# GRU, ternary layer and mixture of experts on one core: first weights in quarters, the first gate's seven products in another order, and matmuls of a constant ahead of them

## The chip, the cores and the metric

The kernel runs on one core of a Trainium2 chip. The metric is device time in microseconds (us) of one execution; three executions of the kernel before gave 2669.57, 2669.85 and 2670.73 us.

## The reference

Two blocks, all in f32. The first runs a GRU over 64 steps of a batch of 128, feeds its states through a layer with ternary weights and adds the input; the second runs a causal convolution whose taps are the conditioning rows, and a mixture of 64 experts with a shared expert. Only the GRU's input product matters here:

```
def cell(h, x):                       # x: 128 x 512, one step
    gi = x @ W_ih + b_ih              # 512 -> 1536: gates r, z, n
    gh = h @ W_hh + b_hh
    r = sigmoid(i_r + h_r); z = sigmoid(i_z + h_z)
    n = tanh(i_n + r * h_n)
    return (1 - z) * n + z * h
x = x + ffn(scan(cell, cond, x))      # ffn: ternary 512 x 512 weight
x = x + moe(conv(x, taps = cond))
```

## The kernel before

**The input product.** `x @ W_ih` is not multiplied out as it stands. Two steps t and t+1 are taken together, and their two 512-wide rows against the 512 columns of one gate are a 2 by 2 block product, done with seven block products (Winograd's form of Strassen) instead of eight. The blocks of x are `x11, x12` (step t, first and second half of the features) and `x21, x22` (step t+1). The blocks of a gate's weights are `w11, w12, w21, w22` (half of the features by half of the columns). One block product, `Chunk.product(n)` at L323, is two f32 matmuls of 128 by 128 by 256, and the profile records each as two, so it is "x4" in the trace, all on L338. Product 1 multiplies x11 and w11. Product 5 multiplies `s1 = x21 + x22` by `t1 = w12 - w11`, product 6 multiplies `s2 = s1 - x11` by `t2 = w22 - t1`, product 7 multiplies `x11 - x21` by `w22 - w12`, product 4 multiplies x22 by `t4 = w21 - t2`, product 3 multiplies `s4 = x12 - s2` by w22, and product 2 multiplies x12 and w21.

**Who makes the sums.** `pair_operands(t)` (L300) makes the four sums of x, on VectorE for the first pair and on GpSimd for all others. `prepare(c)` (L281) makes the four sums of gate c's weights and adds the two biases of the gate together (L294), on VectorE.

**Where the results go.** There are four PSUM tiles, `psx, psy, psw, psz`, one buffer each. Product 1 begins psx and product 2 adds to it; 7 begins psw and 4 adds to it; 5 begins psz and 3 adds to it; 6 has psy. VectorE reads each after its product: `p1` = product 1 plus the bias (L353), `u2` = product 6 plus p1 (L356), `u3` = product 7 plus half of u2 (L359), then the four quarters `gi` of the result (L361, 363, 365, 367). So product 2 can only start when p1 has been read out of psx, product 4 only when u3 has been read out of psw, and p1 needs the bias.

**The order of the work.** `input_gates()` (L369) yields one product at a time, gate by gate in the order 0, 2, 1 and within a gate in the order 1, 6, 7, 3 of the gate before, 2, 4, 5. The first 24 are taken before the recurrence begins (L448); then each step of the recurrence takes 10 or 11. On TensorE the products of the first pair are held in exactly this order (`issue_after`); all other order on each engine is laid down at build time by a planner with costs of its own, which may move an instruction ahead of others that stand before it in the text.

**The loads.** All early loads go out on SyncE's queue, in the order of the text: x of the first pair (L223, 512 KB), the weights of gate 0 in two halves of the features (L254, 512 KB each), the two biases of gate 0 repeated to 128 rows (L259, L262, 256 KB each), the weights and biases of gates 2 and 1 (1 MB a gate), the first state `h`, x of the second pair, then `whh` (1 MB a gate) and the rest. Each issue takes SyncE about half a microsecond, and each of them waits until the load eight places before it has landed: such a wait shows in the trace on SyncE's queue.

After the 24 products the recurrence runs: per step twelve f32 matmuls of the state with `whh` (L502), the gates on VectorE and ScalarE, the ternary layer of the step before (L417), and products of the pairs ahead in between. Once, ahead of the first of these layers, VectorE turns the ternary weights into signs (L457 to L471), for which `wf` must have landed.

Of the kernel before, what the change touches and what calls it, by code (L numbers as in the profile page):

```python
# [8 lines left out]
F32 = mybir.dt.float32  # L9
# [5 lines left out]
ALU = mybir.AluOpType  # L15
# [4 lines left out]
P = 128  # L20
B = 128
T = 64
D = 512
# [19 lines left out]
def adaln_ffn_kernel(  # L43
# [156 lines left out]
    with (  # L200
# [21 lines left out]

        load_pair(0, nc.sync)  # L223
        h = el0.tile([P, D], F32, name="h")
# [16 lines left out]
        bi = wi.tile([P, 3 * D], F32, name="bi")  # L241
        wih = [wi.tile([P, KD, D], F32, name=f"wih{c}") for c in range(3)]

# [7 lines left out]

        for h_ in range(2):
            half_ = slice(h_ * HD, (h_ + 1) * HD)
            load_rows(wih[0][:, h_ * HK : (h_ + 1) * HK], w_ih[half_, cols[0]])  # L254
        bh = {}
        for c in (0, 2, 1):
            if c:
                load_rows(wih[c], w_ih[:, cols[c]])
            repeated(bi[:, cols[c]], b_ih[cols[c]])  # L259
            if c != 2:  # L260
                bh[c] = el0.tile([P, D], F32, name="r")
                repeated(bh[c], b_hh[cols[c]])  # L262
        nc.sync.dma_start(out=h, in_=cond)
        load_pair(2, nc.sync)
# [10 lines left out]
        nc.vector.memset(ones, 1.0)  # L275

        wsum = {}

        def prepare(c):  # L281

            w = wih[c]
            w11, w12 = w[:, :HK, :HD], w[:, :HK, HD:]
            w21, w22 = w[:, HK:, :HD], w[:, HK:, HD:]
            t1 = wi.tile([P, HK, HD], F32, name=f"t1{c}")
            nc.vector.tensor_sub(t1, w12, w11)
            t2 = wi.tile([P, HK, HD], F32, name=f"t2{c}")
            nc.vector.tensor_sub(t2, w22, t1)  # L289
            nc.vector.tensor_sub(w12, w22, w12)  # L290
            t4 = wi.tile([P, HK, HD], F32, name=f"t4{c}")
            nc.vector.tensor_sub(t4, w21, t2)
            if c in bh:
                nc.vector.tensor_add(bi[:, cols[c]], bi[:, cols[c]], bh[c])  # L294
            wsum[c] = {1: w11, 2: w21, 3: w22, 4: t4, 5: t1, 6: t2, 7: w12}

        gis, last = {}, []
        made = []

        def pair_operands(t):  # L300

            xp = xps.pop(t)
            x11, x12 = xp[:, 0, :HK], xp[:, 0, HK:]
            x21, x22 = xp[:, 1, :HK], xp[:, 1, HK:]
            s = xpp.tile([P, 3, HK, B], F32, name="xs")
            s1, s2, s4 = s[:, 0], s[:, 1], s[:, 2]
            engine = nc.gpsimd if t else nc.vector
            engine.tensor_add(s1, x21, x22)
            engine.tensor_sub(s2, s1, x11)
            engine.tensor_sub(x21, x11, x21)  # L310
            engine.tensor_sub(s4, x12, s2)
            return {1: x11, 2: x12, 3: s4, 4: x22, 5: s1, 6: s2, 7: x21}

        class Chunk:


            def __init__(self, t, c, ops):
                self.c, self.ops, self.ws = c, ops, wsum[c]
                self.g = [gip.tile([P, 2, HD], F32, name="gi") for _ in range(2)]
                gis[t, c], gis[t + 1, c] = (g.rearrange("p h d -> p (h d)") for g in self.g)  # L320
                self.ps = {}

            def product(self, n):  # L323
# [33 lines left out]
                elif n == 7:  # L357
                    self.u3 = gtp.tile([P, HD], F32, name="u3")
                    add(self.u3, ps, self.u2[:, 1])  # L359
                elif n == 5:  # L360
                    add(g1[:, 1], ps, self.u3)  # L361
# [7 lines left out]
        def input_gates():  # L369
# [1111 lines left out]
```

## Time and profile before

| what | value |
|---|---|
| median of three runs (lowest, highest) | 2669.85 us (2669.57, 2670.73) |
| the profiled execution's own time | 2670.76 us |
| its span, first to last instruction | 2669.0 us |
| TensorE busy with matmuls | 2639.1 us, 99% |
| VectorE, ScalarE, GpSimd busy | 1412.3, 426.3, 458.0 us |
| first product of the input (L338) starts | 5.99 us |
| first matmul of the recurrence (L502) starts | 34.26 us |

The profile is of one execution. Its page shows the busy time of each engine, and the trace can be asked for the instructions of a stretch in order of time (the timeline), for the busy time of each engine in given stretches (the windows), and for the chain of waits that ended last. In a timeline row stand the start and the length in us, the engine, the line of the kernel, the operation, what it writes and reads, the shape, and how many instructions were merged; in brackets how long the engine stood idle before and what ended it. "PEld" is the load of the stationary operand, "SPq" is SyncE issuing a transfer. The ends of matmuls are modelled, so that rows of TensorE overlap a little.

### The profile page before, as it was taken

Reading aid. Unit: us, or ns where it says so; the run is one execution under the profiler, and the core shown is the slowest. Engines: PE = TensorE matmul, PEld = TensorE weight load, DVE = VectorE, ACT = ScalarE, POOL = GpSimd, SP = SyncE. Lnnn points to the kernel's source line nnn. Section 1 sums busy time; section 2 is a strip of 40 time slices with the busy share of each in tenths; the row PEclk is TensorE's granted clock in tenths of the full one; section 3 lists DMA queues with packets and bytes.
Section 4 is the critical chain, followed back from the end, with each engine's and each line's share of the span. In section 5 each row is a group of like instructions: output and inputs, shape, how many; then the busy total and the mean of one; then the engine's idle time right before and its main releaser. Section 6 shows DMA issues by size and latency. Waiting matters only on the chain.

```text
span 2669.0 us, 31315 instructions
## 1 busy us (share of the span) xinstructions
PE 2639.1 (99%) x11959; PEld 1818.0 (68%) x11959; DVE 1412.3 (53%) x3148; ACT 426.3 (16%) x795; POOL 458.0 (17%) x534
## 2 busy tenths in 40 slices
PE   8999999999999999999999999999999999999999
PEld 5666666666666666666658667777876666666667
DVE  6555555555555555555547655566574343434334
ACT  1111111111111111111110222222221111111111
POOL 2112121111112111211114100000001222222210
PEclk9999999999999999999999999999999999999999
DMA  5323332332322222322228811222256899998962
GB/s 193 69 56 63 57 67 57 58 61 53 60 47 51 44 52 44 75 45 58 48 67 294 324 25 26 39 61 60 61 169 174 287 305 294 288 330 262 293 182 48
DMA packets 476054, 323.35 MB, mean 121 GB/s; under 512 B 329472, under 2 KB 395648, under 8 KB 473728
## 3 DMA queue, kind: packets, MB, share of 16 engines
q1 hardware_dynamic: 447312, 248.18, 33.3%
q0 software_dynamic: 28592, 73.16, 11.3%
q8 instruction: 95, 1.56, 0.2%
q14 instruction: 55, 0.45, 0.1%
HBM read 235.01 MB, written 92.55 MB: 123 GB/s over the span
## 4 chain that ended last, share of the span: by engine, by line
PE 93%; issue 2%; DMA 2%; DVE 2%; ACT 0%; SPq 0%; POOL 0%; DVEq 0%; POOLq 0%; ACTq 0%
PE psgh L502 25%; PE psz L695 7%; PE psw L695 7%; PE psx L695 6%; PE psw L338 6%; PE psz L338 6%; PE psx L338 6%; PE psf L417 4%; PE py L1370 3%; PE y L695 3%; PE psy L338 3%; PE pg L1344 3%; PE pu L1344 3%; PE psc L182 2%; PE y L869 1%
## 5 line engine op out<-in xcount | busy, mean ns | idle before, releaser
L502 PE MATMUL psgh<-whh,hT 128*128 128x512 f32 x1536 | 676.3, 597 | 0.7 <-ACT hT L399 0.7
L502 PEld LDWEIGHTS psgh<-whh,hT 128*128 128x128 f32 x1536 | 287.5, 190 | 351.0 <-issue 336.9
L338 PE MATMUL psx<-wih,xp 128*128 128x256 f32 x768 | 198.5, 381 | 6.4 <-DMA wih<-in_w_ih_dram 6.0
L220 POOL DMA_DIRECT2D xn<-in_x_dram x61 | 33.9, 555 | 842.4 <-DVE x L428 830.8
L338 PEld LDWEIGHTS psx<-wih,xp 128*128 128x128 f32 x768 | 143.8, 191 | 25.6 <-issue 6.0
L512 DVE TENSOR_TENSOR n<-psgh,bhn 128x512 f32<-128x512 f32 x64 | 44.2, 691 | 175.2 <-PE psgh L502 175.2
L1353 DVE SCALAR_TENSOR_TENSOR a<-a,rw,pu 128x352 f32<-128x352 f32 x32 | 18.6, 580 | 215.1 <-PE pu L1344 215.1
L399 ACT COPY hT<-psf 128x512 f32<-128x512 f32 x64 | 37.5, 585 | 584.2 <-PE psf L393 584.2
L509 DVE TENSOR_TENSOR r<-psgh,gi 128x512 f32<-128x512 f32 x64 | 44.2, 691 | 142.5 <-PE psgh L502 142.5
L413 POOL TENSOR_TENSOR xn<-xn,fb 128x512 f32<-128x512 f32 x64 | 80.8, 1263 | 144.1 <-DMA xn<-in_x_dram 144.1
L338 PE MATMUL psz<-wih,xs 128*128 128x256 f32 x384 | 98.7, 380 | 1.8 <-DVE gi L361 1.8
L338 PE MATMUL psy<-t,xs 128*128 128x256 f32 x384 | 99.9, 383 | 0.4 <-DVE t L289 0.3
L338 PE MATMUL psw<-t,xp 128*128 128x256 f32 x384 | 98.8, 380 | 0.4 <-DVE u L359 0.4
L338 PE MATMUL psw<-wih,xp 128*128 128x256 f32 x384 | 98.8, 380 | 0.0
L338 PE MATMUL psz<-t,xs 128*128 128x256 f32 x384 | 98.7, 379 | 0.0
L417 PE MATMUL psf<-sgn,hhi 128*128 128x512 f32 x256 | 95.1, 493 | 0.3 <-DVE hlo L407 0.3
L1370 PE MATMUL py<-wd,aeT 128*64 128x512 f32 (+1 forms) x384 | 89.5, 601 | 0.0
L353 DVE TENSOR_TENSOR p<-psx,bi 128x512 f32<-128x512 f32 x96 | 66.4, 691 | 37.5 <-PE psx L338 37.2
L515 ACT ACTIVATE n<-n 128x512 f32<-128x512 f32 x64 | 40.3, 629 | 274.0 <-DVE n L514 274.0
L695 PE MATMUL psx<-hid,swg 128*128 128x256 f32 x320 | 83.7, 384 | 0.3 <-ACT g L735 0.3
L695 PE MATMUL psx<-xr,swg 128*128 128x256 f32 x320 | 83.6, 383 | 0.0
L356 DVE TENSOR_TENSOR u<-psy,p 128x512 f32<-128x512 f32 x96 | 66.3, 691 | 29.4 <-PE psy L338 29.1
(306 smaller groups left out, 4678.4 us busy)
## 6 DMA issues: line engine op xcount, KB each, us to landing
wg<-in_w_gate_dram SPq DMA_DIRECT2D x64, 704.0 KB, 9.6
wu<-in_w_up_dram SPq DMA_DIRECT2D x64, 704.0 KB, 11.0
wd<-in_w_down_dram SPq DMA_DIRECT2D x64, 512.0 KB, 7.0
x1c<-x SPq DMA_DIRECT2D x62, 256.0 KB, 5.2
out_dram<-x SPq DMA_DIRECT2D x62, 256.0 KB, 5.4
xn<-in_x_dram POOLq DMA_DIRECT2D x61, 256.0 KB, 4.1
xp<-in_xT_dram POOLq DMA_DIRECT2D x30, 512.0 KB, 5.2
xc<-x1c SPq DMA_DIRECT2D x28, 512.0 KB, 8.3
```

The costliest lines, as they stand in the source:

```text
L182: i = nc.tensor.matmul(ps[rows, j].rearrange("p h (u t) -> p h u t", u=2), xcs[sl % NCB][:, rows, g * 4 + j], tzs[sl % NCB][:, :, :, g * 4 ...
L338: i = nc.tensor.matmul(ps, self.ops[n][:, k, :], self.ws[n][:, k, :], start=(first and k == 0), stop=(k == HK - 1), skip_group_check=not f ...
L353: add(self.p1, both, b)
L356: add(self.u2, both, self.p1)
L413: nc.gpsimd.tensor_add(xn, xn, fb)
L417: nc.tensor.matmul(ps, piece[:, k, :], sgn[:, k, :], start=(i == 0 and k == 0), stop=(i == 1 and k == KD - 1),)
L502: nc.tensor.matmul(ps, hT[:, k, :], whh[c][:, k, :], start=(k == 0), stop=(k == KD - 1))
L509: nc.vector.tensor_add(r, ps_r, gis.pop((t, 0)))
L512: nc.vector.tensor_add(n, ps_n, bhn)
L695: i = nc.tensor.matmul(ps.rearrange("p (j b) -> p j b", b=P) if len(r.shape) == 3 else ps, lhs(k), r, start=(first and k == 0), stop=(k == ...
L1344: nc.tensor.matmul(acc[halves[j]], self.xeT[:, k, halves[j]], self.ws[j][which][:, k, :], start=(k == 0), stop=(k == KD - 1),)
L1370: nc.tensor.matmul(py[halves[j]], self.aeT[:n, c, halves[j]], self.ws[j][2][:n, c, :], start=(c == 0), stop=(c == len(ech) - 1),)
```

## The change

Four edits, all of them at the start of the kernel.

1. The loads that gate 0 needs go out in nine pieces in place of five: x11 (128 KB), w11 (256 KB), x of the second step (256 KB), w12, w22 (256 KB each), the two biases, x12 (128 KB), w21 (256 KB). The four quarters of gate 0's weights are tiles of their own, `wb`. Biases now stand ahead of x12 and w21. Everything behind keeps its order.
2. Seven 128 by 128 by 128 matmuls of `ones` with itself are put ahead of the first product. Nothing reads their result.
3. In the first gate the products run in the order 1, 5, 6, 7, 2, 4. As product 5 now comes before u3 exists, its PSUM tile is kept (`p5`), and the quarter that used to be added at product 5 is added behind u3 at product 7.
4. VectorE's sums for that gate are held in the order s1, t1, s2, t2, x11 - x21, w22 - w12, the bias, s4, t4, where the four sums of x came first before.

```diff
-        load_pair(0, nc.sync)
+        xps[0] = xpp.tile([P, 2, KD, B], F32, name="xp")
...
-        for h_ in range(2):
-            half_ = slice(h_ * HD, (h_ + 1) * HD)
-            load_rows(wih[0][:, h_ * HK : (h_ + 1) * HK], w_ih[half_, cols[0]])
+        def load_block(k, n):
+            load_rows(wb[k, n], w_ih[k * HD : (k + 1) * HD, n * HD : (n + 1) * HD])
...
+        nc.sync.dma_start(out=xps[0][:, 0, :HK], in_=xT[0, :, :HK])
+        load_block(0, 0)
+        nc.sync.dma_start(out=xps[0][:, 1], in_=xT[1])
+        load_block(0, 1)
+        load_block(1, 1)
+        load_biases(0)
+        nc.sync.dma_start(out=xps[0][:, 0, HK:], in_=xT[0, :, HK:])
+        load_block(1, 0)
+        for c in (2, 1):
+            load_rows(wih[c], w_ih[:, cols[c]])
+            load_biases(c)
...
+        ps = ps_f.tile([P, D], F32, name="psf")
+        for _ in range(7):
+            nc.tensor.matmul(ps[:, :P], ones, ones, start=True, stop=True)
...
+            todo = [
+                (t1, w12, w11, ALU.subtract),
+                (t2, w22, t1, ALU.subtract),
+                (w12, w22, w12, ALU.subtract),
+                (t4, w21, t2, ALU.subtract),
+            ]
             if c in bh:
-                nc.vector.tensor_add(bi[:, cols[c]], bi[:, cols[c]], bh[c])
+                b = bi[:, cols[c]]
+                todo.insert(3, (b, b, bh[c], ALU.add))
+            if c == 0:
+
+                x1, x2, x7, x4 = xsums
+                todo = [x1, todo[0], x2, todo[1], x7, *todo[2:4], x4, todo[4]]
+            for operands in todo:
+                with tc.issue_after(summed[-1].ins) if c == 0 and summed else nullcontext():
+                    summed.append(nc.vector.tensor_tensor(*operands))
...
                 elif n == 7:
                     self.u3 = gtp.tile([P, HD], F32, name="u3")
                     add(self.u3, ps, self.u2[:, 1])
+                    if self.p5 is not None:
+                        add(g1[:, 1], self.p5, self.u3)
+                elif n == 5 and "psw" not in self.ps:
+                    self.p5 = ps
                 elif n == 5:
                     add(g1[:, 1], ps, self.u3)
...
-                    for n in (1, 6, 7, 3, 2, 4, 5):
+                    for n in (1, 6, 7, 3, 2, 4, 5) if prev else (1, 5, 6, 7, 2, 4):
```

More of the change, by code (lines that the diff above doesn't have):

```diff
@@ L241, in adaln_ffn_kernel @@
         bi = wi.tile([P, 3 * D], F32, name="bi")
-        wih = [wi.tile([P, KD, D], F32, name=f"wih{c}") for c in range(3)]
+        wb = {
+            (k, n): wi.tile([P, HK, HD], F32, name=f"w{k}{n}") for k in range(2) for n in range(2)
+        }
+        wih = {c: wi.tile([P, KD, D], F32, name=f"wih{c}") for c in (1, 2)}
         xc0 = xcs[0].rearrange("p b e -> p (b e)")
@@ L248, in repeated, with load_biases @@
             nc.sync.dma_start(out=dst, in_=row.partition_broadcast(P))
-        for h_ in range(2):
-            half_ = slice(h_ * HD, (h_ + 1) * HD)
-            load_rows(wih[0][:, h_ * HK : (h_ + 1) * HK], w_ih[half_, cols[0]])
+        def load_block(k, n):
+            load_rows(wb[k, n], w_ih[k * HD : (k + 1) * HD, n * HD : (n + 1) * HD])
         bh = {}
-        for c in (0, 2, 1):
-            if c:
-                load_rows(wih[c], w_ih[:, cols[c]])
+        def load_biases(c):
             repeated(bi[:, cols[c]], b_ih[cols[c]])
@@ L275, in adaln_ffn_kernel @@
         nc.vector.memset(ones, 1.0)
+        ps = ps_f.tile([P, D], F32, name="psf")
+        for _ in range(7):
+            nc.tensor.matmul(ps[:, :P], ones, ones, start=True, stop=True)
         wsum = {}
         def prepare(c):
[L283 to L292, printed above, removed]
-            if c in bh:
-                nc.vector.tensor_add(bi[:, cols[c]], bi[:, cols[c]], bh[c])
+            if c == 0:
+                w11, w12, w21, w22 = (wb[k, n] for k in range(2) for n in range(2))
+            else:
+                w = wih[c]
+                w11, w12 = w[:, :HK, :HD], w[:, :HK, HD:]
+                w21, w22 = w[:, HK:, :HD], w[:, HK:, HD:]
+            t1, t2, t4 = (wi.tile([P, HK, HD], F32, name=f"t{n}{c}") for n in (1, 2, 4))
+            todo = [
[4 more added lines that the diff above has]
+            ]
+            if c in bh:
+                b = bi[:, cols[c]]
+                todo.insert(3, (b, b, bh[c], ALU.add))
+            if c == 0:
+                x1, x2, x7, x4 = xsums
[3 more added lines that the diff above has]
+                    summed.append(nc.vector.tensor_tensor(*operands))
             wsum[c] = {1: w11, 2: w21, 3: w22, 4: t4, 5: t1, 6: t2, 7: w12}
         gis, last = {}, []
-        made = []
+        made, summed, xsums = [], [], []
         def pair_operands(t):
@@ L306, in pair_operands @@
             s1, s2, s4 = s[:, 0], s[:, 1], s[:, 2]
[L307 to L311, printed above, removed]
+            todo = [
+                (s1, x21, x22, ALU.add),
+                (s2, s1, x11, ALU.subtract),
+                (x21, x11, x21, ALU.subtract),
+                (s4, x12, s2, ALU.subtract),
+            ]
+            if t == 0:
+                xsums.extend(todo)
+            else:
+                for operands in todo:
+                    nc.gpsimd.tensor_tensor(*operands)
             return {1: x11, 2: x12, 3: s4, 4: x22, 5: s1, 6: s2, 7: x21}
@@ L320, in __init__ @@
                 gis[t, c], gis[t + 1, c] = (g.rearrange("p h d -> p (h d)") for g in self.g)
-                self.ps = {}
+                self.ps, self.p5 = {}, None
             def product(self, n):
```

## The prediction

> **What bounds the kernel now.** The page comes first: its table of engines and its slices say whether a gain at the start can reach the end.
>
> ```profile
> PE 2639.1 (99%) x11959; PEld 1818.0 (68%) x11959; DVE 1412.3 (53%) x3148; ACT 426.3 (16%) x795; POOL 458.0 (17%) x534
> ...
> PE   8999999999999999999999999999999999999999
> ```
>
> TensorE is without matmuls for 2669.0 - 2639.1 = 30 us in all, and its first slice is the weakest. So the start is a fair target, and what TensorE gains there comes out at the end unless another engine takes it back. The profiled execution took 2670.76 us, 1.8 over its span and 0.9 over the median of the runs; I count in its trace and take the difference off the median.
>
> The timeline of the first 15 us comes next, to see what TensorE waits for.
>
> ```profile
> 5.94 0.68 DVE L287 TENSOR_TENSOR t<-wih 128x512 f32<-128x512 f32 x1
> ...
> 5.99 2.05 PE L338 MATMUL psx<-wih,xp 128*128 128x256 f32 x4 [5.99 <-DMA wih<-in_w_ih_dram]
> ...
> 8.33 2.07 PE L338 MATMUL psy<-t,xs 128*128 128x256 f32 x4 [0.29 <-DVE t L289]
> ...
> 10.40 0.69 DVE L294 TENSOR_TENSOR bi<-bi,r 128x512 f32<-128x512 f32 x1 [0.93 <-DMA r<-in_b_hh_dram]
> ...
> 11.94 1.13 PE L338 MATMUL psx<-wih,xp 128*128 128x256 f32 x4 [0.37 <-DVE p L353]
> ...
> 13.27 1.13 PE L338 MATMUL psw<-t,xp 128*128 128x256 f32 x4 [0.19 <-DVE u L359]
> 14.24 1.03 PE L338 MATMUL psz<-t,xs 128*128 128x256 f32 x4
> ```
>
> Two things are seen. A product takes 2.05 us at first and 1.03 later (0.86 from one to the next): TensorE starts at half its rate. And what ends the last waits is not the weights: the bias lands at 10.3, and behind it stand four steps on VectorE, one after the other (bias 10.40, p1 11.20, u2 11.99, u3 12.79), before product 4 may start at 13.27. The chain of waits says the same of the bias:
>
> ```profile
> 2.83 7.48 DMA r<-in_b_hh_dram
> ```
>
> Last the windows, for who is the bound behind that point.
>
> ```profile
> 10.00:15.00 5.00, 4.44 (x17) 3.19 (x17) 3.99 (x8) 0.00 (x0) 0.00 (x0) 1.00 1.05 399
> 15.00:20.00 5.00, 5.00 (x24) 4.10 (x23) 5.00 (x10) 0.00 (x0) 0.00 (x0) 1.00 1.05 367
> 20.00:25.00 5.00, 5.00 (x24) 4.07 (x22) 4.67 (x8) 0.00 (x0) 3.72 (x4) 1.00 1.05 391
> ```
>
> After the stretch stand TensorE, its weight loads, VectorE, ScalarE, GpSimd, the clock, the busy share of the DMA engines and GB/s. From 15 to 25 VectorE is as full as TensorE (5.00 and 4.67 of 5), and so are the DMA engines. That decides my forecast.
>
> **Part by part.** *Smaller loads.* The same 2 MB go out ahead of gate 2's weights as before. The first issue is at 0.81, the next ones half a microsecond apart, so nine issues last until 0.81 + 9 x 0.5 = 5.3; the DMA engines move 256 KB in about 0.7 us (360 to 400 GB/s), so they are not starved. Product 1 needs 384 KB instead of the 1024 KB that landed at 5.85. In the trace x's 512 KB had landed at 4.4, and w11 is issued second, at 1.31: I take 4.1 for it, between 3.5 (384/512 of the bytes behind a start at 1.8) and 5.85 (nothing gained). w12 and w22 follow at 0.7 us each, some 5.6 and 6.3. The price is the length of the runs: quarters of the weights and halves of x move in runs of 1 KB. The trace's packet records have 84 ns as the median for 2 KB and 48 for 1 KB, so 1 KB costs 6 ns more per KB on each of 16 engines: for 1280 KB that is 1280 x 6 / 16 = 0.5 us on everything behind. It lies in the slack of later loads (the wait for `wf` ends at 36.6, and VectorE stands idle there because the result is only wanted with the matmuls that end at 41.3).
>
> The page "DMA: Bandwidth & Descriptors" of the Trainium skill (section Bandwidth) speaks against small pieces: batch transfers to 1 MiB, as 1 MB reaches 341 GB/s and 64 KB only 138. By it a 256 KB piece would get some 240 GB/s (an estimate between the page's two figures), and the bias would land 2 us later, not earlier. The windows decide against it: with transfers of 256 KB to 1 MB queued behind one another the rows above have 367 to 399 GB/s.
>
> *The bias.* It now has 1152 KB ahead of it instead of 1536. At 390 GB/s that is 1.0 us earlier, less 0.3 for the runs of 1 KB: 9.65 instead of 10.31. The bounds are 8.6 and 10.8, since the trace's window rows show only 90 to 119 GB/s from 7.5 to 9.0, while the bias moves; whether this belongs to the bias or to the moment isn't shown.
>
> *Seven matmuls of ones.* `ones` is written at 0.91 and ready at 1.1. A product's 256 columns start 0.43 us apart at the slow rate, so 128 columns take 0.21: 14 records x 0.21 = 3.0 us, 1.15 to 4.15. They end about where w11 lands, so they cost nothing if it lands at 4.1, and at most 0.6 if it lands at 3.5. What they bring is product 1, 5, 6 or 7 at the full rate. But all four stand ahead of a wait for the bias, so even slow ones are done in time: 4.2 + 1.7, then 5 from 6.4 (t1), 6 and 7, 1.7 each, to 11.5. I take nothing for it, and 0.9 as the most (one product at the full rate).
>
> *The order 1, 5, 6, 7, 2, 4.* Product 5 no longer follows product 4, which takes 0.86 us of TensorE out of the stretch behind 13.27. The four products that need no bias are done by about 9.2 at the full rate (5 behind t1 at 6.3, 6 behind t2 at 7.4, 7 behind w22 - w12 at 8.3). Then TensorE waits for p1. In place of a wait for weights there is one for the bias of some 2 us, and queued behind product 2 are all the products of gate 2.
>
> *VectorE.* s4 and t4 used to be done before the bias came; now x12 and w21 land behind it, and the two sums cost 0.34 + 0.60 = 0.94 us behind it. That is the hidden price. With the bias at 9.65 the chain to u3 ends 0.66 earlier, at 12.6. The two sums go in behind it or into it, so VectorE stands where it stood before at 13.5 instead of 13.2: -0.66 + 0.94 = 0.28 later. It wins back the 0.29 that it waited for product 4 at 14.44. Sum for VectorE: 0.0. The added sum for product 5 replaces one that was there.
>
> *The sum.* TensorE is ahead by 0.86 + 0.66 = 1.5 us when gate 2 begins. If VectorE, full from 15 to 25, hands on u3 of gate 1 at 25.9 as before, nothing of it is left at the product that waits for it at 26.37. If TensorE's lead is kept, 1.5 is. The row nearest is VectorE's 5.00 of 5.00, but it also holds 1.0 us in which two of its sums took 1.12 and 1.21 instead of 0.68, beside GpSimd's, and that can move either way. I take the middle, -0.7: 2669.85 - 0.7 = 2669.1 us. About 0.2% (5.3 us) is what a measurement of this kernel can tell from no change, and this is far less.
>
> **The rivals.** *A: the wait for the bias throws the clock back.* The trace has one such place, in the windows at the end of the recurrence:
>
> ```profile
> 1390.00:1391.00 1.00, 0.00 (x0) 0.00 (x0) 1.00 (x3) 0.00 (x0) 0.00 (x0) 1.00 0.00 0
> 1391.00:1392.00 1.00, 0.45 (x4) 0.42 (x4) 0.50 (x1) 0.00 (x0) 0.00 (x0) 1.00 0.08 8
> 1392.00:1393.00 1.00, 0.32 (x3) 0.12 (x2) 0.00 (x0) 0.72 (x2) 0.00 (x0) 1.00 0.87 91
> ...
> 1394.00:1395.00 1.00, 1.00 (x2) 0.33 (x1) 0.21 (x1) 0.00 (x0) 0.00 (x0) 0.50 0.85 130
> ```
>
> Waits of 1.65 and 0.68 us close together, with TensorE busy for 0.77 of 3 us (26%), were followed by 3.4 us at half the clock, a loss of 1.7 us. The new kernel has a wait of some 2.2 us from 9.2 to 11.4. It decides if TensorE is busy for a quarter or less of the stretch the clock is judged by; with products 6 and 7 in front I count 35 to 50%. The price is 1.7 for one period: 2669.85 - 0.7 + 1.7 = 2670.9, slower than before, and 2672.6 with two.
> The page "TensorE: Matmul & The Clock Gate" of the Trainium skill (sections What you observe, HAM oscillation) says full clock comes after about 3.4 us of steady work, is judged in windows of that length that run freely, and is lost by idle gaps over 3.4 us. By it this wait would be harmless; the rows above show a loss after 1.65 and 0.68, so I keep the rival.
>
> *B: the front comes through whole.* If the biases move at the 390 GB/s of the rows around them, they land 1.0 us earlier still; then TensorE's lead is 2.5 us, and if the planner uses it to shorten the 1.8 us wait of psz for VectorE at 49.7, 4.3. That gives 2669.85 - 2.5 = 2667.3 to 2665.5. Against it stands VectorE's full row; past -5.3 it would need more of the waits behind 13.27 to go.
>
> *C: the planner lays the rest out anew.* The order on every engine comes from its costs, and the start shifts them. The price is that of the waits there are behind 14 us: 30 - 6.0 - 1.0 = some 23 us, in pieces of up to 1.8. Three such pieces more or fewer are 5.4: 2664.5 or 2675.3. Nothing in the profile tells the sign.
>
> *D: no smaller waits.* If the pieces land together, as the queue interleaves them, product 1 starts near 5.9 still, and 0.5 us of short runs remain: 2670.3.
>
> **How the numbers follow.** Forecast 0.36; A 0.14 (0.03 of it past +0.2%); B 0.20 (half of it past -0.2%); C 0.24 (0.05 faster, 0.09 slower past the bound); D 0.06. Faster by over 0.2%: 0.10 + 0.05 = 0.15. Slower: 0.03 + 0.09 = 0.12. Within: 0.73. The range leaves out some 0.09 on each side: past B's and C's lower ends by one more piece of 1.8, 2663.0, and past C's upper end by the half microsecond of short runs, 2676.0. The forecast's own range is -1.5 - 0.9 to +0.6: 2667.4 to 2670.5.
>
> **What would show it.** Right: product 1 at full rate near 4.2; products 1, 5, 6, 7 done near 9.2; a bias step on VectorE near 9.7; product 4 near 13 and gate 2's first product near 14 instead of 14.9; and then VectorE full to 26, with the first matmul of the recurrence within 1.5 us of 34.26. The forecast is wrong if L502 starts before 32.5, if a row of the first 20 us has a clock of 0.50 behind product 7, or if the traces part behind 35 us by more than they did there.

## The result, and the profile after

The changed kernel takes 2674.2 us (median of 18 runs, 2671.19 to 2677.79), the kernel before, run beside it, 2670.25 (18 runs, 2667.65 to 2673.29). The ratio is 1.0015, with a 95% interval of 1.0009 to 1.0021. It is slower, by some 4 us. That is inside the 0.2% that I set as the bound of a difference, but the interval excludes no change, and the forecast was 0.7 us faster.

The profiled execution took 2675.57 us, its span is 2673.9. Its page begins with the table of engines:

```profile
PE 2643.0 (99%) x11973; PEld 1819.2 (68%) x11973; DVE 1409.6 (53%) x3148; ACT 426.7 (16%) x795; POOL 457.5 (17%) x534
```

TensorE has 14 instructions more, the matmuls of ones. It starts 4.9 us earlier and is still without matmuls for 30.9 us (2673.9 - 2643.0), where it was for 30: the idle time has come back elsewhere. The timeline of the start shows where:

```profile
1.13 3.35 PE L294 MATMUL psf<-ones 128*128 128x128 f32 x14 [1.13 <-DVE ones L290]
...
4.28 1.75 PE L374 MATMUL psx<-w,xp 128*128 128x256 f32 x4
...
6.95 1.13 PE L374 MATMUL psz<-t,xs 128*128 128x256 f32 x4 [0.92 <-DVE t L324]
...
8.86 1.10 PE L374 MATMUL psw<-w,xp 128*128 128x256 f32 x4
...
10.67 0.69 DVE L324 TENSOR_TENSOR bi<-bi,r 128x512 f32<-128x512 f32 x1 [1.90 <-DMA r<-in_b_hh_dram]
...
11.28 0.41 DVE L324 TENSOR_TENSOR xs<-xp,xs 128x256 f32<-128x256 f32 x1
11.61 0.68 DVE L389 TENSOR_TENSOR p<-psx,bi 128x512 f32<-128x512 f32 x1
...
12.21 0.68 DVE L324 TENSOR_TENSOR t<-w,t 128x512 f32<-128x512 f32 x1
...
12.35 1.92 PE L374 MATMUL psx<-w,xp 128*128 128x256 f32 x4 [2.39 <-DVE p L389]
...
12.81 0.68 DVE L392 TENSOR_TENSOR u<-psy,p 128x512 f32<-128x512 f32 x1
13.60 0.42 DVE L395 TENSOR_TENSOR u<-psw,u 128x256 f32<-128x256 f32 x1
...
14.08 2.04 PE L374 MATMUL psw<-t,xp 128*128 128x256 f32 x4
```

Product 1 starts at 4.28, 5 at 6.95, 7 at 8.86 as meant, though product 1 doesn't have the full rate yet (1.75 us). Then TensorE stands for 2.39 us. The bias step on VectorE comes at 10.67, not at 9.65 and not even at 10.40 as before; between it and u3 now stand s4 (11.28) and t4 (12.21). And product 2 takes 1.92 us instead of 1.13: the clock has gone. The chain of waits still names the same transfer:

```profile
3.73 6.85 DMA r<-in_b_hh_dram
```

The clock is granted in stretches that begin and end on a grid of 3.41 us; the trace lists them, and where the grid lies differs from one execution to the next. The windows, asked for on this execution's grid (after the stretch: length, busy TensorE, weight loads, VectorE, ScalarE, GpSimd, clock, DMA share, GB/s):

```profile
5.72:9.13 3.41, 2.49 (x11) 1.65 (x10) 2.56 (x5) 0.00 (x0) 0.25 (x1) 1.00 0.55 208
9.13:12.55 3.42, 1.03 (x5) 0.58 (x4) 1.88 (x4) 0.00 (x0) 0.00 (x0) 1.00 1.03 388
12.55:15.96 3.41, 3.41 (x9) 2.35 (x9) 2.72 (x6) 0.00 (x0) 0.00 (x0) 0.50 1.05 388
15.96:19.37 3.41, 3.07 (x15) 2.41 (x14) 3.11 (x6) 0.00 (x0) 0.00 (x0) 1.00 0.94 297
```

In the second row TensorE is busy for 1.03 of 3.42 us, 30%; the third row then has half the clock although TensorE is full in it. Such a stretch is called a fall from here on.

A second place differs, near 49 us, inside the first step of the recurrence. It is the wait of psz for VectorE that rival B had its eye on. The timelines of TensorE there, before and then after:

```profile
42.84 0.28 PE L462 MATMUL psf<-total,ones 128*128 128x1 f32 x2
42.98 1.96 PE L502 MATMUL psgh<-whh,hT 128*128 128x512 f32 x4
...
49.72 1.10 PE L338 MATMUL psz<-wih,xs 128*128 128x256 f32 x4 [1.76 <-DVE gi L361]
```

```profile
44.58 0.28 PE L502 MATMUL psf<-total,ones 128*128 128x1 f32 x2
44.72 1.10 PE L542 MATMUL psgh<-whh,hT 128*128 128x512 f32 x2
...
51.46 1.10 PE L374 MATMUL psz<-w,xs 128*128 128x256 f32 x4 [2.62 <-DVE gi L401]
```

`psf<-total` sums the absolute ternary weights over the partitions; VectorE's signs wait for it, and VectorE's work for the products waits behind the signs. The planner has put that small matmul behind one more matmul of the recurrence: 4 records (two matmuls) stood behind it before, 2 (one) now. VectorE is that much later, and the wait grew from 1.76 to 2.62 us.

### The profile page after: what moved, and what is told of

It is laid out like the page before. It is cut to its first block, busy times and chain, and to the rows that moved or that the text cites. A ratio compares the mean times of both kernels' runs of the same rounds, so it can differ in the third digit from the quotient of the medians.

```text
span 2673.9 us, 31354 instructions
## 1 busy us (share of the span) xinstructions
PE 2643.0 (99%) x11973; PEld 1819.2 (68%) x11973; DVE 1409.6 (53%) x3148; ACT 426.7 (16%) x795; POOL 457.5 (17%) x534
## 4 chain that ended last, share of the span: by engine, by line
PE 92%; DMA 3%; DVE 2%; issue 2%; ACT 0%; SPq 0%; POOL 0%; DVEq 0%; POOLq 0%; ACTq 0%
PE psgh L542 25%; PE psz L735 7%; PE psw L735 7%; PE psx L735 6%; PE psw L374 6%; PE psz L374 6%; PE psx L374 6%; PE psf L457 4%; PE py L1410 3%; PE y L735 3%; PE psy L374 3%; PE pg L1384 3%; PE pu L1384 3%; PE y L909 1%; PE psf L433 1%
## 5 line engine op out<-in xcount | busy, mean ns | idle before, releaser
L374 PE MATMUL psx<-wih,xp 128*128 128x256 f32 x512 | 131.5, 379 | 0.0
L374 PEld LDWEIGHTS psx<-wih,xp 128*128 128x128 f32 x512 | 97.3, 190 | 13.8 <-DVE p L389 0.4
L550 ACT ACTIVATE r<-r 128x512 f32<-128x512 f32 x64 | 40.3, 630 | 260.9 <-DVE r L549 260.9
L374 PEld LDWEIGHTS psw<-t,xp 128*128 128x128 f32 x384 | 73.1, 191 | 12.2 <-DVE u L395 1.1
```

The lines of the kernel that those rows point to most:

```text
L374: i = nc.tensor.matmul(ps, self.ops[n][:, k, :], self.ws[n][:, k, :], start=(first and k == 0), stop=(k == HK - 1), skip_group_check=not f ...
L550: nc.scalar.activation(r, r, AF.Sigmoid)
```

## The experiments

All are read by the same marks in the profile: the bias step on VectorE, product 2, the first matmul of the recurrence, `psf<-total`, the first matmul of the third step, and the stretches of half clock ahead of 1390 us. Times in us; the median of the runs stands beside the ratio to the kernel before (11 runs of each kernel, 18 for the first row of after; single runs have no ratio).

| kernel | bias | product 2 | recurrence | total | third step | half clock from | median | ratio (95%) |
|---|---|---|---|---|---|---|---|---|
| before | 10.40 | 11.94 | 34.26 | 42.84 | 77.32 | none | 2670.25 | 1 |
| b_again | 10.02 | 11.56 | 33.84 | 42.43 | 76.91 | none | 2669.47 | 0.9996 (0.9987 to 1.0005) |
| b_again2 | 10.31 | 12.01 | 34.06 | 42.65 | 77.11 | none | 2668.11 (one) | |
| after | 10.67 | 12.35 | 35.14 | 44.58 | 79.06 | 12.55 | 2674.2 | 1.0015 (1.0009 to 1.0021) |
| e0_again | 10.72 | 12.41 | 34.71 | 44.15 | 79.69 | 51.41 | 2674.4 | 1.0012 (1.0003 to 1.0021) |
| a_p3 | 11.06 | 12.75 | 36.05 | 45.49 | 81.05 | 15.04, 52.59 | 2675.53 (one) | |
| a_p4 | 10.76 | 12.45 | 34.20 | 43.64 | 78.12 | none | 2673.52 (one) | |
| e1_fill | 10.32 | 12.03 | 33.77 | 43.21 | 77.71 | none | 2672.26 | 1.0008 (0.9999 to 1.0017) |
| u_warm | 10.84 | 12.52 | 34.28 | 43.72 | 78.21 | none | 2672.87 | 1.001 (1.0 to 1.0019) |
| u_loads | 10.57 | 12.86 | 35.22 | 42.95 | 77.43 | none | 2670.65 | 0.9999 (0.999 to 1.0008) |
| e3_bias | 12.24 | 15.20 | 35.74 | 42.61 | 77.59 | 7.78 (twice as long) | 2671.97 | 1.0005 (0.9996 to 1.0014) |
| e4_bias_pe | none | 11.31 | 31.41 | 40.93 | 76.06 | none | 2673.21 | 1.001 (1.0001 to 1.0019) |
| e2_two | 10.98 | 12.66 | 34.44 | 43.13 | 82.23 | 14.49, 52.03 | 2674.68 | 1.0013 (1.0004 to 1.0022) |
| e2_three | 10.97 | 12.65 | 33.64 | 43.18 | 82.34 | 12.36, 53.32 | 2676.14 | 1.0015 (1.0006 to 1.0024) |
| e6_fill_both | 11.14 | 12.83 | 34.58 | 44.03 | 78.50 | none | 2671.26 | 1.0002 (0.9993 to 1.0011) |
| b_fill2 | 10.27 | 12.11 | 33.71 | 42.29 | 76.78 | none | 2669.82 | 1.0 (0.9991 to 1.0009) |
| e5_defer | none | 13.03 | 32.74 | 43.12 | 75.43 | 8.66 | 2668.89 | 0.9995 (0.9986 to 1.0004) |
| b_defer | 10.07 | 11.62 | 33.84 | 44.14 | 74.31 | none | 2668.62 | 0.9992 (0.9983 to 1.0001) |

The kernel before, run beside them, had medians of 2670.58, 2670.63, 2670.58 and 2670.77 in the four groups of runs. The medians of equal kernels differ by 1.1 us (b_again against the kernel beside it), so what is worth less than that is read from the marks. The half clock is given as the trace lists it; where no row is shown, the windows show it in the same way as above.

The mean granted clock of every single execution is on record too, rounded to thousandths. One fall takes half of 3.41 us, 0.0006 of the span, so 0.999 stands for one or two falls and 0.998 for two or more, the one at the end of the recurrence included. In the four later groups the kernel before has 1.000 in 49 of 114 executions (median 2669.84) and 0.999 in the other 65 (2671.28). The changed kernel (after and e0_again together) never has 1.000: 0.999 in 12 executions (2673.06), 0.998 in 17 of 29 (2674.76).

### The changed kernel again: e0_again, a_p3, a_p4

No edit.

> The changed kernel once more, for what scatters from one execution to the next. Its profile had the clock at half from 12.55 to 15.96 us, the first matmul of the recurrence (psgh) at 35.14 against 34.26 before, the third step's at 79.06 against 77.32, and another 2.7 us between 1441 and 1530. Theory: the first 1.7 us (to the third step) belong to the change and come again within 0.3, except that the half clock may fall elsewhere, since the stretch that it is judged by need not begin at the same place; the 2.7 us are scatter and need not come again. Rival: the 2.7 us belong to the change and come again within 0.3. Time against the kernel before: +2 to +5 us either way.

> The changed kernel, a third profile. Theory: a half clock behind the wait for the bias or behind the one near 49 us; third step at 78.7 to 80.0; from the first psc to the first pst of the 21st group 132.3 to 136.1 (kernel before: 132.3 to 133.4 in three profiles), so overlapping. Rival: 134.4 or more in every profile.

> The changed kernel, a fourth profile, with the same expectations.

The clock was thrown back at the first wait in one execution (after), at the wait near 49 in one (e0_again), at both in one (a_p3) and at neither in one (a_p4). The windows on the grids of e0_again and of a_p4:

```profile
48.00:51.41 3.41, 0.79 (x4) 0.39 (x4) 3.41 (x8) 1.23 (x2) 0.00 (x0) 1.00 0.15 36
51.41:54.82 3.41, 3.41 (x10) 2.66 (x9) 3.41 (x8) 0.63 (x1) 0.00 (x0) 0.50 0.06 14
```

```profile
8.73:12.14 3.41, 1.54 (x7) 0.87 (x5) 1.73 (x4) 0.00 (x0) 0.00 (x0) 1.00 1.04 375
12.14:15.55 3.41, 2.51 (x10) 1.92 (x11) 3.27 (x8) 0.00 (x0) 0.00 (x0) 1.00 1.04 385
46.27:49.69 3.42, 1.64 (x8) 1.11 (x6) 3.42 (x7) 0.20 (x1) 0.00 (x0) 1.00 0.16 38
49.69:53.10 3.41, 2.49 (x9) 1.62 (x10) 3.41 (x8) 1.66 (x3) 0.00 (x0) 1.00 0.09 20
```

a_p4 has the same waits, 2.17 and 2.62 us. But its grid cuts both in two, and no window falls under 1.54 of 3.41 (45%). The third step was expected at 78.7 to 80.0 and came at 81.05 and 78.12: two falls and none. In e0_again the first wait is another: the full clock came only at 10.45, in spite of the matmuls of ones, so products 5 and 6 took 2.08 and 1.78 us and the wait for the bias was 0.84. The stretch behind the recurrence was expected to overlap with the kernel before, or else to be 134.4 or more in every profile; with 134.2 and 134.9 neither came out whole (below).

e0_again shows one more thing: no fall at the front, but its recurrence starts 0.51 later than a_p4's, with the bias step at the same time. VectorE's timelines, of e0_again and then of a_p4, say where:

```profile
22.48 1.23 DVE L324 TENSOR_TENSOR bi<-bi,r 128x512 f32<-128x512 f32 x1
23.64 1.21 DVE L324 TENSOR_TENSOR t<-wih,t 128x512 f32<-128x512 f32 x1
```

```profile
22.52 0.69 DVE L324 TENSOR_TENSOR bi<-bi,r 128x512 f32<-128x512 f32 x1
23.12 1.22 DVE L324 TENSOR_TENSOR t<-wih,t 128x512 f32<-128x512 f32 x1
```

Beside GpSimd's sums, two of VectorE's are stretched in e0_again and one in a_p4, and the 0.54 us pass through to the recurrence. All three profiles of before have two (the first by 0.44, 0.42 and 0.34), and so has a_p3 (by 0.31).

With that taken out, the way from the bias step to the first matmul of the recurrence is 23.40 to 23.42 us in the three profiles of before and 23.44 in the two of after without a fall at the front (e0_again, a_p4), as it is, to 0.01, in e1_fill, u_warm and e6_fill_both further down. Against 23.44 a fall at the front costs 1.03 (after: 35.14 - 10.67 - 23.44) and 1.24 (a_p3). From there to the third step it is 43.92 where no fall lies near 49, and 44.98 and 45.00 where one does: 1.06 and 1.08. From the recurrence's start to `total` it is 9.44 in all four, and 8.58 or 8.59 before: 0.86 by the planner.

### Keeping TensorE busy in the wait: e1_fill

```diff
+                            if t == 0 and c == 0 and n == 2:
+                                for _ in range(10):
+                                    with tc.issue_after(made[-1].ins):
+                                        made.append(
+                                            nc.tensor.matmul(ps[:, :P], ones, ones, start=True, stop=True)
+                                        )
```

> Ten more matmuls of ones between product 7 and product 2 of the first gate, so that TensorE isn't idle while it waits for the bias. Theory (wait and clock): no half clock behind 10 us; products 2 and 4 at 0.9 to 1.1 us instead of 1.9 and 2.0; the first psgh 0.8 to 1.7 us earlier than in the changed kernel, so 33.4 to 34.3; the time 1 to 2 us below the changed kernel's. Rival (VectorE is the bound from 15 to 25 us, as I forecast): the clock holds, but the first psgh stays at 35.1 within 0.2 and the time does not move.

```profile
9.80 2.39 PE L426 MATMUL psf<-ones 128*128 128x128 f32 x20
12.03 1.11 PE L374 MATMUL psx<-w,xp 128*128 128x256 f32 x4
13.74 1.13 PE L374 MATMUL psw<-t,xp 128*128 128x256 f32 x4 [0.60 <-DVE u L395]
```

Products 2 and 4 run at 1.11 and 1.13 instead of 1.92 and 2.04, there is no fall, and the median is 2.1 us under e0_again in the same group of runs. The matmuls add work and take time away, so what they repair is the clock; the record of the single executions says the same, with 0.998 in 2 of 11. Against the kernel before, run beside it, 1.7 us are left.

### Which edit makes the wait: u_warm, u_loads

u_warm has no matmuls of ones at the start (`range(0)` for `range(7)`); everything else is the changed kernel. u_loads has the loads of the kernel before (x in one load, gate 0's weights in two halves of the features) with the other three edits.

> The changed kernel without its seven matmuls of ones; the planner leaves the order of everything else as it was. Theory (the warming makes the wait that loses the clock): products 1, 5, 6, 7 run at half rate, 1.7 us each, and end near 11.5 instead of 9.7; the wait for p1 shrinks to 1 us, no half clock comes behind full clock before 20 us, products 2 and 4 run at the full rate or nearly, first psgh at 33.7 to 34.7 instead of 35.14 and 34.71, the time 0 to 1.5 us below the changed kernel's. Rival (warming is what holds the front up): slow products delay u2 and u3, first psgh at 35.5 or later, the time 1 us above.

> The changed kernel with the loads of the kernel before (x whole, gate 0's weights in two halves of the features, then the biases); warming, product order and VectorE's order stay, the transposes of the first state are held behind the 24 products. Theory: product 1 at 5.9, product 5 near 6.8, the bias at 10.3 as before, so the wait between product 7 and product 2 is there too (products 1, 5, 6, 7 done by 9.7, product 2 at 12.3) and the first psgh comes at 34 to 35: the loads are not what costs. Rival (the loads cost: runs of 1 KB, the bias 0.3 us later): first psgh at 33.5 or earlier and the time at or under the kernel before.

u_warm:

```profile
8.81 1.91 PE L374 MATMUL psy<-t,xs 128*128 128x256 f32 x4
10.52 1.69 PE L374 MATMUL psw<-w,xp 128*128 128x256 f32 x4
12.52 1.13 PE L374 MATMUL psx<-w,xp 128*128 128x256 f32 x4 [0.32 <-DVE p L389]
```

Left at half rate, products 5, 6 and 7 last until the bias is there: the wait is 0.32 instead of 2.39, product 2 starts within 0.2 us of the same time, and the clock holds from 11.85 on. The median is 1.3 under the changed kernel, little more than the 1.1 between equal kernels, but the clock is 0.999 in all 11 executions, where the changed kernel had 0.998 in 17 of 29. So the matmuls of ones bring nothing, as predicted, and in many executions they cost: they let the products end early, and the wait that this makes is what throws the clock back. The wait near 49 (2.6 us) is still there, and a fall at it was not met in this profile.

u_loads has a wait of 2.20 us too, for the same bias, so the small loads alone don't make it. There VectorE makes s4 and t4 both ahead of p1, which puts product 2 2.29 us behind the bias step instead of 1.68. Its product 1 is 1.7 us later than in after, and its recurrence starts at 35.22, but the planner put `psf<-total` 7.73 us behind that instead of 9.44, and the third step is at 77.43. It equals the kernel before, and this says more of that one placement than of the loads. No run has the old order of products or of VectorE's sums with the new loads, so edits 3 and 4 weren't taken apart.

### The bias: e3_bias, e4_bias_pe

In e3_bias the two bias loads go out right behind w11. In e4_bias_pe they are two rows of 2 KB, and one matmul of ones over these 2 rows both adds them and spreads them over 128 rows. Both hold the transposes of h behind the products, an order that the planner may change without that.

```diff
         load_block(0, 0)
+        brow = w0.tile([2, D], F32, name="brow")
+        nc.sync.dma_start(out=brow[0:1], in_=b_ih[cols[0]].unsqueeze(0))
+        nc.sync.dma_start(out=brow[1:2], in_=b_hh[cols[0]].unsqueeze(0))
...
-        load_biases(0)
...
+                                    made.append(
+                                        nc.tensor.matmul(psb, ones[0:2], brow, start=True, stop=True)
+                                    )
+                                    nc.scalar.copy(bi[:, cols[0]], psb)
```

> The changed kernel with the biases of gate 0 loaded right behind w11 instead of behind w22, and the transposes of the first state held behind the 24 products (where they stand in the changed kernel). Theory (the wait for the bias is what breaks the front): the bias step on VectorE at 7 to 8.5 us instead of 10.7, product 2 started by x12 and w21 at 10.5 to 11, no wait of TensorE over 1.7 us behind product 5, no half clock behind 10 us; first psgh 0.7 to 1.7 us earlier than the changed kernel's 35.14, so 33.4 to 34.4. Rival: the bias loads move at some 100 GB/s wherever they stand, so x of the second step, w12 and w22 land 2 us later each, products 5, 6 and 7 with them, and the first psgh stays at 35.1 within 0.3.

> The changed kernel with gate 0's two biases not repeated to 128 rows by the load: two rows of 2 KB are loaded, and one matmul of ones over those two rows puts their sum in PSUM behind product 1, from where ScalarE copies it. VectorE's bias sum for that gate goes, 512 KB of loads go. Theory: x12 and w21 land near 9, products 1, 5, 6, 7, 2, 4 follow each other with no wait over 1 us behind product 5; gate 2's first product starts between 11.5 and 13.5 instead of 15.9; first psgh at 32 to 33.5; time 1.5 to 3 us below the changed kernel's. Rival (VectorE is full from there on): gate 2's first product comes early but the first psgh not before 34.3.

Why is the bias later though 384 KB fewer stand ahead of it? Where the biases move, the DMA engines carry little more than 100 GB/s. Before that is at 7 to 9 us (211 and 102 GB/s), in the changed kernel at 7 to 9 too, and in e3_bias it moves with them to 4 to 6 (windows of after, then of e3_bias):

```profile
7.00:8.00 1.00, 1.00 (x5) 0.74 (x6) 1.00 (x3) 0.00 (x0) 0.00 (x0) 1.00 0.25 100
8.00:9.00 1.00, 1.00 (x6) 0.74 (x6) 0.77 (x2) 0.00 (x0) 0.00 (x0) 1.00 0.56 205
```

```profile
4.00:5.00 1.00, 1.00 (x6) 0.91 (x5) 0.00 (x0) 0.00 (x0) 1.00 (x2) 1.00 0.58 100
5.00:6.00 1.00, 0.41 (x2) 0.01 (x1) 0.00 (x0) 0.00 (x0) 0.96 (x1) 1.00 0.99 100
```

In e4_bias_pe, where gate 0 has no repeated load, no microsecond from 2 to 9 is under 219 GB/s:

```profile
6.00:7.00 1.00, 1.00 (x3) 0.50 (x2) 0.61 (x2) 0.00 (x0) 0.00 (x0) 1.00 1.10 313
7.00:8.00 1.00, 1.00 (x5) 0.53 (x4) 1.00 (x3) 0.47 (x1) 0.00 (x0) 1.00 0.88 240
8.00:9.00 1.00, 1.00 (x6) 0.86 (x5) 1.00 (x3) 0.11 (x1) 0.00 (x0) 1.00 0.89 332
```

So most of the slowness belongs to these loads and not to the moment, which the prediction had left open. Not all of it: in halves of a microsecond e4_bias_pe has 141 and 135 GB/s from 3.5 to 4.5 us, and e5_defer, with the same loads, 115 and 82. Why the biases take longer than before isn't told by this alone; the landings further down say a little more.

In e3_bias all that stands behind the biases comes late (VectorE's first sum at 8.92, product 5 at 10.50), which is worse at the front: the recurrence starts at 35.74, later than the theory and the rival had it. Only the early placement of `psf<-total` (6.87 us behind the first matmul of the recurrence) brings the third step back to 77.59, and the median, 2671.97, with it.

e4_bias_pe has the front that the change was supposed to bring: product 2 at 11.31 behind a wait of 1.01, gate 2's first product at 13.96, no fall, and the third step 1.05 us ahead of the mean of before. The recurrence's start at 31.41 flatters it, as 1.5 products (1.3 us) had been put behind it. The runs didn't follow: 2673.21, in two groups, 2670.75 to 2672.33 and 2673.21 to 2675.22. The expected time was missed. Part of the loss is the clock, which is 0.999 in the quicker executions but for one and 0.998 or 0.997 in six others. The front isn't the same in each execution either: e5_defer, which has it too, shows product 2 at 13.03 and a fall at 8.66. The rest is open; in the profile, of one of the quicker executions, the stretch behind the recurrence is the longer one again.

### The place of `psf<-total`: e2_two, e2_three

In both, `psf<-total` is held by hand behind two or three of the third gate's four matmuls, and the products of the first step behind all four. This takes three products out of the stretch ahead of the recurrence, so that its start can't be compared with the other rows.

> The changed kernel with the one matmul that adds up the ternary weights' size (psf<-total) held behind two psgh matmuls of the third gate, where it stood before the change; the products of the stream that the planner puts beside it are held behind all psgh of the first step. To be read against e2_three. Theory: that matmul starts 0.8 to 0.9 us earlier than in e2_three, the signs on VectorE too, TensorE's wait for gi behind it is shorter by as much (1.8 against 2.6), and so is everything from the second step on: 0.85 us less time. Rival: VectorE's chain of signs isn't what TensorE waits for, and the two differ by less than 0.3 us at the third step.

> The same with that matmul held behind three psgh matmuls of the third gate, where the planner put it in the changed kernel. Theory: 0.85 us more than e2_two at the third step and in the time. Rival: within 0.3 of e2_two.

From the first matmul of the recurrence to `total` it is 8.69 against 9.54, and to the second step 27.36 against 28.29: one matmul later costs 0.93 us there, as expected. The third step shows none of it (82.23 against 82.34), since the fronts happened to differ by 0.8 the other way. Both have two falls, and their third step is 1.2 us later than a_p3's, which has two as well; what holding the products adds to this can't be told apart. TensorE's longest wait there is 2.7 us in the one and 3.5 in the other. The pair supports the price only with the front taken off.

### The wait near 49: e6_fill_both, b_fill2

e6_fill_both is e1_fill with 8 more matmuls of ones ahead of product 3 of the second pair's gate 2, where the wait near 49 stands. b_fill2 is the kernel before with 6 at its own wait there.

> e1_fill (ten matmuls of ones in the wait for the bias) with eight more in the wait of 2.6 us for gi near 49 us. Theory (the half clock that follows a wait is what most of the loss is, and which wait it follows differs from one execution to the next): no half clock before 1390 us in the profile; first psgh at 33.8, third step's at 77.7 within 0.3, as in e1_fill's profile; the time 0.3 to 1.5 us under e1_fill's and within 1 us of the kernel before. Rival (the rest of the loss lies behind the recurrence): the time stays at e1_fill's +1.7 within 0.5.

> The kernel before with six matmuls of ones in its wait of 1.8 us for gi near 49 us. Theory: that wait brings the half clock in few executions or in none, so the time moves by less than 0.7 us. Rival: it brings it in most, and the time falls by 1 to 1.7 us.

```profile
48.13 1.95 PE L434 MATMUL psf<-ones 128*128 128x128 f32 x16
50.91 1.10 PE L374 MATMUL psz<-w,xs 128*128 128x256 f32 x4 [0.84 <-DVE gi L401]
```

With both waits filled no fall is left ahead of 1390, six of the 11 executions have a clock of 1.000, and the median is 2671.26: 3 us under the changed kernel, and not distinguishable from the kernel before. The marks come 0.8 later than expected, as the bias does (11.14 against 10.32 in e1_fill). In the kernel before the same filling changes nothing. Its wait of 1.76 us leaves at least 48% of a window busy (1.65 of 3.41), and no fall was met there in any profile.

### The best version: e5_defer, b_defer

The twelve operations that make the signs, `psf<-total` among them, are written behind the first step of the recurrence instead of ahead of it; e5_defer has this on top of e4_bias_pe, b_defer alone on the kernel before.

```diff
+        def signs():
+            ps_s = ps_f.tile([P, D], F32, name="psf")
...
         for t in range(T):
...
+            if t == 0:
+                signs()
```

> e4_bias_pe with the ternary signs (from psf<-total on) written behind the first step of the recurrence, so that the planner puts VectorE's reads of the first psgh ahead of them. Theory: TensorE's wait of 1.8 to 2.6 us for gi near 50 us goes, and the half clock that can follow it; the third step starts 2 to 3.5 us earlier than in e4_bias_pe, and the time is under the kernel before by 2 to 5 us. Rival: the signs are then late for the first ternary layer and the wait comes back there: no gain at the third step.

> The kernel before with that edit alone. Theory: the wait of 1.8 us near 49.7 goes, the third step's first psgh comes 1.5 to 2.5 us before 77.32, and the time is 1.5 to 2.5 us under the kernel before. Rival: as above, no gain at the third step.

The third step comes at 75.43 and 74.31, against 77.11. The wait near 49 is gone in both, and in b_defer TensorE waits for nothing from 30 to 80 us. e5_defer falls short of what was expected: its third step is 0.6 us ahead of e4_bias_pe's and not 2 to 3.5, as its front was the slower one with a fall, and its median is 1.7 under the kernel before. b_defer's third step is 2.8 ahead, more than expected, and it is the quickest kernel of all, 2 us under the kernel before; its interval, 0.9983 to 1.0001, just touches no change. None of the four edits of the change is in it.

### The kernel before again: b_again, b_again2

> The kernel before, once more, for a second profile and a measure of what two equal kernels differ by. Theory: 0 within 0.7 us; third step at 77.3 within 0.2, or 79.0 if the half clock follows the wait near 49; from the first psc to the end 1254.1 to 1256.5 us (changed kernel: 1256.95 and 1255.4 in two profiles), so that the stretch behind the recurrence scatters by more than the two kernels differ there.

> The kernel before, a third profile, with the same expectations.

These give the spread that the rest is held against: the third step within 0.4 us, where 0.2 was expected, the median 1.1 under its equal, where 0.7 was, and no half clock ahead of 1390. Behind the recurrence lies what is not settled. From the first matmul that counts the experts' rows (`psc`) to the 41st record of the transposes (`pst`) it is 133.4, 133.0 and 132.3 us in the profiles of before, and 136.1, 134.5, 134.2 and 134.9 in those of after. Part of it is one wait, here of before and then of after; it is 0.8 to 1.2 us in the three profiles of before and 1.2 to 2.0 in the four of after:

```profile
PE pst L982 <- DVE hid L992: 1.2, 1, 1.2
```

```profile
PE pst L1022 <- DVE hid L1032: 1.6, 1, 1.6
```

But the order of the instructions there is the same in both kernels, b_fill2 and b_defer, which have the old start, show 134.2 and 135.0, and e1_fill, which has the new one, 133.2. So I can't put this down to the change. It may be scatter in the gathers and scatters of that stretch; that wasn't shown.

A third place of the clock lies just ahead, at the end of the recurrence. From the third step to the first `psc` it is 1337.6 to 1338.0 us in the profiles of before and after with a fall near 1393, and 1336.2 in the one without (b_again2). All four profiles of after have it, and two of the three of before; b_fill2 and b_defer don't. Whether the change makes it more frequent or the grid happened to lie so, these few profiles don't tell.

## Why the prediction was wrong, point by point

The steps that failed are two. The sum had the bias land 0.66 us earlier, and it came 0.56 later; and it put the planner's order and the clock at nothing, which cost 0.86 and 1.10. The points follow one by one.

**Right.** Product 1 starts at 4.28 (predicted 4.1 to 4.2), and nothing was gained by its being early; but it took 1.35 to 1.98 us in the four profiles and not the full rate's 1.03. The wait that takes the place of the one for weights: "some 2 us", 2.39 measured. The matmuls of ones bring nothing; that they cost nothing either was wrong (u_warm). The range holds the time, though not for its reason: its upper end stood for three more waits of 1.8 us, and what came was one of 0.86 beside a late bias and the clock.

**The bias, mis-sized with its sign.** Its step on VectorE was to come at 9.65, 0.66 earlier. It comes at 10.67 to 11.06, on the means 0.56 later than before (10.80 against 10.24). The part that I had counted is there: the last weights ahead of the biases land at 6.79, 7.14 and 7.15 in the three profiles of after that show landings, where it was 7.48, 7.21 and 7.59 before, some 0.4 earlier. But from there to the landing of the second bias it is now 3.52 to 3.83 us, where it was 2.63 to 2.83. I took 390 GB/s for the bytes that no longer stand ahead, and let the biases' own slow rows, 90 to 119 GB/s, stay as they were; instead they last a microsecond longer. u_loads, with the old loads and the other three edits, has 2.74 there, so the new loads are what lengthens it. Whether it is the shorter runs or the two pieces that now follow the biases, no run shows. The small loads are a little slower themselves, too: from 2 to 6 us the four profiles of after move 278 to 306 GB/s, the three of before 321 to 339.

**s4 and t4, priced too high.** VectorE's term of 0.0 was 0.66 won with the bias, 0.94 lost with the two sums, and 0.29 won back. Measured are 0.56 lost with the bias and 0.03 from there to the recurrence, 0.59 in all. The two sums stand inside the chain that ends last: bias, s4, p1, t4, u2, u3. They cost 0.54 there, 3.35 us to the end of u3 against 2.81, because steps that wait for one another started 0.80 apart on VectorE before, and the sums now fill part of these gaps. And two waits of VectorE for TensorE are gone that it had before, 0.29 and 0.23:

```profile
11.20 0.69 DVE L353 TENSOR_TENSOR p<-psx,bi 128x512 f32<-128x512 f32 x1
...
11.99 0.69 DVE L356 TENSOR_TENSOR u<-psy,p 128x512 f32<-128x512 f32 x1
12.79 0.42 DVE L359 TENSOR_TENSOR u<-psw,u 128x256 f32<-128x256 f32 x1
...
14.44 0.42 DVE L365 TENSOR_TENSOR gi<-psw,u 128x256 f32<-128x256 f32 x1 [0.29 <-PE psw L338]
...
21.60 0.42 DVE L361 TENSOR_TENSOR gi<-psz,u 128x256 f32<-128x256 f32 x1 [0.23 <-PE psz L338]
```

So from the bias step on, the forecast lost 0.65 and the runs lose 0.03, and this hides half of the bias's miss of 1.22.

**TensorE's lead of 1.5 us when gate 2 begins.** There is none: gate 2's first product starts at 15.94, 15.10, 15.83 and 15.14, against 15.10, 14.71 and 15.01 before. Nor would a lead have counted. Measured from the bias step, gate 2 begins 0.32 earlier where no fall lies at the front (4.38 against 4.70), and at the recurrence nothing of it is left: 23.44 against 23.40 to 23.42. In a_p4 VectorE waits for no other engine between 10.76 and 27.49. So VectorE's full row was the bound, and of the two values between which I took the middle, none of the lead was the right one.

**Rival A, given 0.14, happened at its own place in two of the four profiles,** and near 49, which I hadn't looked at for the clock at all, in two. Its price was too high there: a fall costs 1.03 to 1.24, where 1.7 was set; part of the half clock lies where VectorE is the bound. Its condition was wrong in the other direction. I asked for TensorE busy for a quarter or less and counted 35 to 50% for the stretch. Over all 18 traces, as far as 1420 us, every window of the grid with TensorE busy for 39% or less was followed by half the clock (20 windows). Of the windows at full rate none above 50% was, and between 43 and 50% both occur. My 35 to 50% spans the very point that decides, and where a window lies on a wait is a matter of the grid. The way up asks for more: windows at half rate that were busy for up to 84% stayed at half, and those with 88% or more were followed by the full rate. That is why the matmuls of ones brought the clock only at 10.45 in e0_again, whose first two windows were 73 and 77% busy. The Trainium skill, page "TensorE: Matmul & The Clock Gate" (What's actually happening; HAM oscillation), says that the window runs freely and is about 3.4 us: the runs agree, with 3.41 and another phase in each execution. It names idle gaps of over 3.4 us as what loses the clock; here 2.39 and 2.62 were enough, so the busy share of a window decided and not the length of one gap.

**Rival C, given 0.24, happened too, at one place.** `psf<-total` moved behind one more matmul, 0.86 us. Its size was inside the pieces of up to 1.8 that I had counted. Why the planner's costs put it there wasn't looked into.

**The sum that the runs give,** as means over four profiles of after and three of before: the bias +0.56, the way from it to the recurrence +0.03, the stretched sum of VectorE -0.19 (0.21 against 0.40), the planner +0.86, the clock +1.10. That is 2.4 us, and the third step is 2.4 later (79.48 against 77.11). The spans of these profiles differ by 5.2 us, more than the medians of the runs (4.0). Of the other 2.8, 0.7 lies ahead of the first `psc`, where the fall near 1393 is in all four profiles of after and in two of the three of before. The last 2.2 lie behind it and stay open.

## What to carry to other kernels

Look for the transfer at the end of the chain, and ask what it takes itself, not only what stands ahead of it: fewer bytes ahead of the biases didn't bring them earlier. Everything that is made early ahead of such a transfer turns into a wait. On TensorE a wait is more than its length: if it empties most of a window of 3.41 us, it cost 1.0 to 1.7 us more here, and work that starts earlier ahead of a wait that doesn't move makes that more likely. Where a planner lays out the rest, find the one instruction whose place decides the next long wait, and settle that by the text: writing twelve operations later gave the quickest kernel here, 2 us at the edge of what the runs can tell, while the whole new start lost 4.

## What the runs showed of the hardware

- The clock goes by a grid of 3.41 us, whose phase differs by execution. A window with TensorE busy for 39% or less was always followed by 3.41 us at half rate, one at full rate above 50% never; from half rate it took a window of 88% or more to come back. The same program differs by up to 2.9 us at its third step, 2.3 of it by two falls.
- Gate 0's two loads that repeat one row over 128 partitions, 256 KB each, move at little more than 100 GB/s wherever they stand (102 from 8 to 9 us before, 100 from 7 to 8 after, 100 from 4 to 6 in e3_bias); the second lands some 2 us behind the first (1.7 to 2.3). The later ones, between loads of 1 MB, show no more than a dip (246 and 270 GB/s from 17 to 19 us in after). A matmul of ones over the two rows took 1.33 us of TensorE in e4_bias_pe, the sum included.
- VectorE's sum of 128 by 512 takes 0.68 us alone; sums of operands in SBUF (t, bi) took 1.0 to 1.24 beside GpSimd's, while p, which reads PSUM, kept 0.69. How many are hit differs from one execution to the next: one or two, in u_loads three.
